# Two graph layers on one core: divisors of two relations in one reciprocal, asked for and applied at other places

## The chip, the cores and the metric

The kernel runs on one NeuronCore of a Trainium2 chip. The metric is the device time of one execution in microseconds. PE is the matrix engine, DVE the vector engine, ACT the scalar engine, POOL the GpSimd engine, and SP the engine whose queue issues most of the loads. Matmuls write into eight PSUM banks; what they leave there is read by ACT or DVE.

## The reference, cut to what matters

Node features of 384 nodes go through a graph attention layer, and then, after a layer norm and a rectification, through a relational network with two convolutions, 768 features, six relations and four bases per convolution. Only the convolution matters here.

```python
W = jnp.einsum('rb,bio->rio', comp, basis)
h_all = jnp.einsum('ni,rio->rno', x, W)
counts = jnp.zeros((R, n), x.dtype).at[edge_type, dst].add(1.0)
norm = 1.0 / counts[edge_type, dst]
msg = h_all[edge_type, src] * norm[:, None]
agg = jax.ops.segment_sum(msg, dst, num_segments=n)
return agg + x @ root + bias
...
x = jax.nn.relu(x)
x = x + h_in
x = _batchnorm(x, bn_gamma[l], bn_beta[l])
```

Each relation's messages are divided by the number of edges of this relation that end in the target node.

## The kernel before

The work stands in one program whose order is written out by hand: PE, POOL, SP, DVE and, after the first projection, ACT take their instructions in the order in which the program names them.

**The adjacency.** The tile `A` holds for each of the six relations a matrix of edge counts, source nodes on the partitions (3 blocks of 128) and 384 target nodes along the row, so that `A[:, r]` has 128 x 1152 numbers. It comes from memory, written there by scatters, relation by relation. For each relation `add_up(r)` on POOL adds the three blocks of sources into `sums[r]`, a slot of `sum_room` (128 x 384). `share(r)` turns this into the divisors. A matmul with a matrix of ones (L411 and L412 in the profile's lines, named `ps_cnt`) adds over the partitions and leaves the count of each target in all 128 partitions. Two ACT instructions (L414, L415) make max(count - 1, 0) + 1 of it, DVE takes the reciprocal (L416) and multiplies `A[:, r]` by it (L417). The divisors alternate between slots 4 and 5 of `sum_room`; the sums use slots 0 to 3, so that `add_up(4)` and `add_up(5)` wait until slots 0 and 1 have been read.

**The mixtures.** `mix(l, r, At, bs)` adds relation r, times its coefficient, onto `At[:, b]` for each basis b. For relation 0 it writes, on ACT (L396); for the others it adds, on DVE (L398). All of it must be done before the aggregation multiplies `At` with the transformed features.

**The bases.** Features times basis b gives `H_[:, b]`. Bases 0 and 1 of layer 0 are multiplied by a scheme of 15 products. Bases 2 and 3 use one of fewer products on halves. For each of them PE first runs three parts c=0, 1, 2 of 12 matmul instructions each (L1245), which fill the banks pe, pf, pb and pa. Then come the products with S[0], S[1], S[3] and S[2], of 6 instructions each (L1239): the S[0] and S[3] products in bank pc, the S[1] and S[2] products added onto bank pa. Between them ACT and DVE read out what has come together so far: ACT copies pa to `hs[0][0]` (L1251) before the S[1] product may add onto it, and again after it (L1258); DVE adds pb (L1252) and later products (L1260, L1262). The last product, `rest`, adds onto pa in part c=0 of the next basis, and ACT reads it (L1266). The sums of weights for the next basis (L1034, L1036) are made on DVE right after L1262, the fourth sum of weights (L1042) after the `rest`. Then follow the root matmuls (L1282), sums of the mixed adjacency (L1142) and of the features (L1365), and the aggregation (L1348), whose results DVE adds onto the features (L1375).

**What is put between.** `go_between(l, b, c)` is called after each part c of basis b, and with c=4 after the basis's products and the next basis's weight sums. What is done there is listed in `between`: shares of relations 0, 1, 2 after the parts of basis 2, share 3 and the mixture of relation 0 at (0, 2, 4), shares 4 and 5 after the first two parts of basis 3, and all mixtures of relations 1 to 5 at (0, 3, 4), ahead of the root matmuls.

**Banks.** `next_bank` takes the bank that was taken longest ago of those allowed. A matmul into a bank waits until what the bank held has been read.

```python
ps = next_bank("ps_cnt", [i for i in range(8) if i not in taken])
...
pe, pf, pb, pc, pa = [next_bank("ps_g", [i for i in range(8) if i not in taken[-1:]])[:, :N]
                      for _ in range(5)]
taken[:] = ring[-5:]
```

For basis 2 these are, by following the ring through the program, banks 3, 4, 7, 5 and 6, so that its pa is bank 6.

**Loads.** The weights of a basis come in three parts of four loads each through five buffers (L135, on SP's queue); the root's three parts (L137) come behind basis 3's. A load waits in the queue until its buffer has been read for the last time.

Of the kernel before, what the change touches and what calls it, by code (L numbers as in the profile page):

```python
# [14 lines left out]
AF = mybir.ActivationFunctionType  # L15
ALU = mybir.AluOpType

P = 128
N = 384
NT = N // P  # L20
# [5 lines left out]
HD = D // H  # L26
# [5 lines left out]
R = 6  # L32
# [69 lines left out]
def gnn_kernel(ctx: ExitStack, tc: tile.TileContext, out, x, edges, chunks, cols, rows, small,  # L102
               wq, wk, wv, wiq, wik, wiv, wo, w_in, basis, thirds, root, root_thirds, w_out):
    nc = tc.nc
# [15 lines left out]
    def next_bank(name, among=range(8)):  # L120

        i = next(i for i in ring if i in among)
        ring.remove(i)
        ring.append(i)
        return bank(i, name)
# [57 lines left out]
    ones = const.tile([P, P], F32, name="ones")  # L183
    nc.gpsimd.memset(ones, 1.0)

    minus = const.tile([P, 1], F32, name="minus")
# [4 lines left out]
    ps = next_bank("ps_warm")  # L191
# [197 lines left out]
    A = None  # L389

    def mix(l, r, At, bs=range(B)):

        for b in bs:
            w = small_sb[:, 4 + (l * R + r) * B + b:][:, :1]
            if r == 0:
                nc.scalar.activation(At[:, b], A[:, r], AF.Identity, scale=w)  # L396
            else:
                nc.vector.scalar_tensor_tensor(At[:, b], A[:, r], w, At[:, b], ALU.mult, ALU.add)  # L398

    sums = {}  # L400
    taken = []

    def add_up(r):
        sums[r] = sum_room[:, r % 4]
        nc.gpsimd.tensor_tensor(sums[r], A[:, r, 0, :], A[:, r, 1, :], ALU.add)
        nc.gpsimd.tensor_tensor(sums[r], sums[r], A[:, r, 2, :], ALU.add)

    def share(r):

        ps = next_bank("ps_cnt", [i for i in range(8) if i not in taken])  # L410
        nc.tensor.matmul(ps[:, :N], ones, sums[r], start=True, stop=True)  # L411
        rn = sum_room[:, 4 + r % 2]  # L412

        nc.scalar.activation(rn, ps[:, :N], AF.Relu, bias=minus)  # L414
        nc.scalar.activation(rn, rn, AF.Identity, bias=ones[:, 0:1])  # L415
        nc.vector.reciprocal(rn, rn)  # L416
        nc.vector.tensor_tensor(A[:, r], A[:, r], rn[:, None, :].to_broadcast([P, NT, N]), ALU.mult)  # L417
        if r + 4 < R:
            add_up(r + 4)


    with ExitStack() as inner:
        ap = inner.enter_context(tc.tile_pool(name="attn", bufs=2))
# [67 lines left out]
        with tc.tile_pool(name="edge", bufs=1, side="right") as ep:  # L491
# [5 lines left out]
            with tc.manual_schedule(engines={mybir.EngineType.Activation}):  # L497
# [6 lines left out]
                half = lambda t: lambda j: x_sb[:, t, j * 512:(j + 1) * 512]  # L504
# [180 lines left out]
        At = late.tile([P, B, NT, N], F32, name="At")  # L685
        A = late.tile([P, R, NT, N], F32, tag="A", name="A")
        sum_room = late.tile([P, 6, N], F32, name="sum_room")
# [206 lines left out]
        for j in range(2):  # L894
            ps = next_bank("ps_y", range(1, 8))[:, :256]
            for k in range(KD):
                nc.tensor.matmul(ps, attT[:, k, 2 * P:], w_o[1][k // 4][:, k % 4, j * 256:(j + 1) * 256],
                                 start=(k == 0), stop=(k == KD - 1))
# [108 lines left out]
    with tc.tile_pool(name="conv", bufs=1) as cp:  # L1007
# [107 lines left out]
        def shares(*rs):  # L1115
            return lambda: [share(r) for r in rs]

        def mixes(l, r, *bs):
            return lambda: mix(l, r, At, bs)

        between = {(0, 2, 0): shares(0), (0, 2, 1): shares(1),
                   (0, 2, 2): shares(2), (0, 2, 4): lambda: [share(3), mix(0, 0, At)],
                   (0, 3, 0): shares(4), (0, 3, 1): shares(5),
                   (0, 3, 4): lambda: [mix(0, r, At) for r in range(1, R)],
                   (1, 0, 0): mixes(1, 0, 0, 1, 2, 3)}
        for i in range(10):
            between[1, (i + 1) // 3, (i + 1) % 3] = mixes(1, 1 + i // 2, *((0, 1), (2, 3))[i % 2])
# [93 lines left out]
        for l in range(L):  # L1221
# [7 lines left out]
            for b in range(0 if l else BY_15, B):  # L1229
# [12 lines left out]
                for c in range(3):  # L1242
                    for ps, n, i, o, first in ((pa, 0, 0, 0, True), (pe, 2, 0, 0, True), (pf, 2, 0, 1, True),
                                               (pb, 0, 1, 0, True), (pe, 2, 1, 0, False), (pf, 2, 1, 1, False)):
                        nc.tensor.matmul(ps, block(XT, n, i)[:, c], w[c][:, i, o * HC:(o + 1) * HC],  # L1245
                                         start=(first and c == 0), stop=(c == 2 and (i == 1 or ps is pa)))
# [33 lines left out]
            for k in () if l else range(KC):  # L1280
                for o in range(KC):
                    nc.tensor.matmul(pr[o], w[k // 2][:, k % 2, o * P:(o + 1) * P], XT[:, k, :], start=(k == 0),  # L1282
                                     stop=(k == KC - 1))
# [73 lines left out]
            def feature_sums(p):  # L1357

                s0, s1, s3 = spaces[p % 2 * 3:][:3]
                o0, o1 = 2 * p, 2 * p + 1  # L1360
                S.append((s0, s1, h(o1, 0), s3))
                for dst, x, y, op in ((s0, h(o1, 0), h(o1, 1), ALU.add), (s1, s0, h(o0, 0), ALU.subtract),
                                      (h(o1, 0), h(o0, 0), h(o1, 0), ALU.subtract),
                                      (s3, h(o0, 1), s1, ALU.subtract)):
                    nc.vector.tensor_tensor(dst, x, y, op)  # L1365
                    yield
# [33 lines left out]
            for p in range(pairs):  # L1400
                last = p == pairs - 1
                sums = iter(()) if last else feature_sums(p + 1)
# [94 lines left out]
        ps = [next_bank("ps_f") for _ in range(3)]  # L1497
# [107 lines left out]
```

## Time and profile before

| what | value |
|---|---|
| runs | 710.24, 716.94 and 717.36 us, median 716.94 us |
| profiled execution | 709.97 us, span 708.2 us, mean granted clock 0.996 |
| PE busy | 691.4 us, 98% of the span |
| DVE busy | 557.9 us, 79% |
| ACT busy | 162.9 us, 23% |
| POOL busy | 313.5 us, 44% |
| count matmuls L411 | 12 instructions, 486 ns median each |
| reciprocals L416 | 6 of 128 x 384, 2.55 us each, 415.7 to 446.2 us |
| shares L417 | 6 of 128 x 1152, 1.36 us each |
| mixtures L398, both layers | 40 of 128 x 1152, 1.41 us each |

The profile is one execution; its times are counted from the start of the span. The span is what lies between the first and the last instruction, and the execution's time is 1.8 us longer. An instruction's own duration can be longer than its share of the path, because successive instructions of an engine overlap a little. Basis 2 of layer 0 begins at 409 us, basis 3 at 431 us, the root at 454.7 us and the aggregation near 480 us.

### The profile page before, as it was taken

What the parts mean: (1) busy time and instruction counts of PE and PEld (TensorE: products, weight loads), DVE (VectorE), ACT (ScalarE), POOL (GpSimd) and SP (SyncE); (2) the same over time, 40 slices, a digit from 0 to 9 for tenths busy, and PEclk for the clock granted to TensorE, in tenths of its full rate; (3) what the DMA queues carried; (4) which work ended last, traced back from release to release, by engine and by line L of the source; (5) the groups of instructions that cost most, each with busy time, mean ns of one, the idle gap of its engine ahead of it and who ended that gap; (6) DMA issues with size and microseconds to landing.
All of it is one profiled execution on the core that took longest, in us unless ns stands there. A gap on an engine that the chain in (4) does not pass through costs nothing.

```text
span 708.2 us, 9470 instructions
## 1 busy us (share of the span) xinstructions
PE 691.4 (98%) x3324; PEld 541.1 (76%) x3324; DVE 557.9 (79%) x1381; ACT 162.9 (23%) x375; POOL 313.5 (44%) x242
## 2 busy tenths in 40 slices
PE   8999999999999999999999999999999999999995
PEld 7759999999997444478998855558975555899943
DVE  6887697968886799787667889798878679378866
ACT  3201111111111577510131124101131111110101
POOL 1366678778687787588786473000000000000004
PEclk9999999999999999999999999999999999999998
DMA  8887677372563622733524996321004223520002
GB/s 305 271 305 261 221 254 211 76 246 60 213 195 59 179 2 2 223 45 46 120 0 91 238 285 190 134 89 45 1 1 131 69 77 124 193 90 1 0 1 90
DMA packets 70478, 91.07 MB, mean 129 GB/s; under 512 B 23084, under 2 KB 52368, under 8 KB 70046
## 3 DMA queue, kind: packets, MB, share of 16 engines
q1 hardware_dynamic: 48414, 79.24, 33.0%
q0 software_dynamic: 21296, 9.60, 10.6%
q10 hardware_dynamic: 720, 1.62, 0.7%
q8 instruction: 26, 0.43, 0.2%
q14 instruction: 22, 0.18, 0.1%
HBM read 79.27 MB, written 11.16 MB: 128 GB/s over the span
## 4 chain that ended last, share of the span: by engine, by line
PE 81%; DVE 13%; ACT 2%; DMA 2%; issue 1%; SPq 0%; DVEq 0%; ACTq 0%
PE ps_k L452 10%; PE ps_g L1245 9%; PE ps_v L452 9%; PE ps_g L1239 8%; PE ps_c L1348 7%; PE ps_q L470 6%; PE ps_q L452 5%; PE ps_g L1095 4%; DVE At L398 4%; PE ps_y L452 3%; PE ps_x L452 3%; PE ps_c L1183 3%; PE ps_o L758 2%; PE ps_s L713 2%; PE ps_pT L747 2%; PE ps_v L636 2%
## 5 line engine op out<-in xcount | busy, mean ns | idle before, releaser
L333 POOL DMA_INDIRECT atab<-count,at x99 | 166.2, 1679 | 49.2 <-DMA atab<-count,at 23.2
L328 POOL DMA_INDIRECT mtab<-m_val,at x99 | 104.6, 1057 | 54.9 <-issue 24.1
L1478 POOL TENSOR_TENSOR hf<-hf,room 128x512 f32<-128x512 f32 x3 | 4.3, 1421 | 257.8 <-ACT hf L1476 257.8
L398 DVE SCALAR_TENSOR_TENSOR At<-A,small_sb,At 128x1152 f32<-128x1152 f32 x40 | 53.6, 1413 | 0.0
L1245 PE MATMUL ps_g<-w_c,XN 128*128 128x384 f32 x144 | 47.7, 487 | 1.1 <-DVE XN L1375 1.1
L470 PE MATMUL ps_q<-hT,w_q 128*128 128x384 f32 (+1 forms) x160 | 41.8, 422 | 1.4 <-ACT hT L151 1.4
L1245 PEld LDWEIGHTS ps_g<-w_c,XN 128*128 128x128 f32 x144 | 27.3, 190 | 20.2 <-DVE XN L1375 1.4
L470 PEld LDWEIGHTS ps_q<-hT,w_q 128*128 128x128 f32 x160 | 28.5, 190 | 14.1 <-ACT hT L151 1.7
L1348 PE MATMUL ps_c<-At,H 128*128 128x192 f32 x216 | 36.7, 326 | 0.0
L1348 PEld LDWEIGHTS ps_c<-At,H 128*128 128x128 f32 x216 | 35.3, 190 | 0.5 <-DVE XN L1375 0.2
L452 PE MATMUL ps_k<-T,S 128*128 128x192 f32 x192 | 35.1, 326 | 0.0
L452 PEld LDWEIGHTS ps_k<-T,S 128*128 128x128 f32 x192 | 31.8, 190 | 0.0
L726 DVE CUSTOM_DVE_ANT_0 s<-ps_s,mask 128x384 f32<-128x384 f32 x48 | 24.5, 549 | 5.1 <-PE ps_s L713 5.1
L317 DVE SCALAR_TENSOR_TENSOR same<-cells,own,later 128x128 f32<-128x128 int32 x99 | 27.9, 348 | 0.4
L317 DVE SCALAR_TENSOR_TENSOR same<-keys,key,weigh 128x128 f32<-128x128 int32 x99 | 27.9, 349 | 0.0
L1239 PE MATMUL ps_g<-room,x_all 128*128 128x384 f32 x72 | 25.2, 486 | 0.0
L1245 PE MATMUL ps_g<-w_c,XT 128*128 128x384 f32 x72 | 24.3, 487 | 0.6 <-DVE H L1101 0.6
L1282 PE MATMUL ps_c<-XT,w_c 128*128 128x384 f32 x72 | 23.5, 486 | 0.0
L758 PE MATMUL ps_o<-At,v 128*64 128x384 f32 x96 | 20.8, 512 | 1.3 <-ACT attT L761 1.3
L713 PE MATMUL ps_s<-k,q 64*128 64x384 f32 x96 | 21.5, 528 | 0.0
L1245 PEld LDWEIGHTS ps_g<-w_c,XT 128*128 128x128 f32 x72 | 13.6, 190 | 10.3 <-DVE H L1101 1.0
L1239 PEld LDWEIGHTS ps_g<-room,x_all 128*128 128x128 f32 x72 | 13.7, 190 | 9.5
(386 smaller groups left out, 1556.7 us busy)
## 6 DMA issues: line engine op xcount, KB each, us to landing
w_c<-in_basis SPq DMA_DIRECT2D x72, 192.0 KB, 4.5
atab<-zero SPq DMA_DIRECT2D x36, 192.0 KB, 4.9
A<-atab POOLq DMA_DIRECT2D x12, 576.0 KB
keys<-keys_d SPq DMA_DIRECT2D x25, 192.0 KB, 5.0
w_c<-in_thirds SPq DMA_DIRECT2D x24, 192.0 KB, 3.6
w_q<-in_wiq SPq DMA_DIRECT2D x16, 256.0 KB, 5.8
w_k<-in_wk SPq DMA_DIRECT2D x16, 256.0 KB, 4.5
w_k<-in_wik SPq DMA_DIRECT2D x16, 256.0 KB, 4.2
```

Of the source, the lines that this page charges most:

```text
L317: nc.vector.scalar_tensor_tensor(same, row[:, n, :], mine[:, c:c + 1], times, ALU.is_equal, ALU.mult, accum_out=count[:, i, c:c + 1])
L328: nc.gpsimd.indirect_dma_start(mtab[c // PER][:, :], bass.IndirectOffsetOnAxis(at[:, 0, c:c + 1], 0), m_val[:, c:c + 1], None)
L333: nc.gpsimd.indirect_dma_start(atab[0 if i < 11 else i % 2][:, :], bass.IndirectOffsetOnAxis(at[:, 1, c:c + 1], 0), count[:, 1, c:c + 1], ...
L398: nc.vector.scalar_tensor_tensor(At[:, b], A[:, r], w, At[:, b], ALU.mult, ALU.add)
L452: nc.tensor.matmul(ps, a[:, k, :], b[:, k, :], start=start and k == 0, stop=(k == 3), skip_group_check=not start)
L470: nc.tensor.matmul(ps[o][:, c], wt_[:, k, o * P:(o + 1) * P], src[:, k, c], start=(k == 0 and c.start == 0), stop=(k == KD - 1 and c.stop ...
L713: nc.tensor.matmul(score[g][j][:, :N], q2[ho, hc, t * P:(t + 1) * P], k2[ho, hc, :], start=True, stop=True)
L758: nc.tensor.matmul(pso[p][j * HD:(j + 1) * HD, :N], v2[:, m, h * HD:(h + 1) * HD], turned(g)[:, j, :], start=(m == 0), stop=(m == NT - 1))
L1095: nc.tensor.matmul(ps, x[:, j], w[:, j], start=start and j == 0, stop=(j == 2), skip_group_check=not start)
L1239: nc.tensor.matmul(ps, x[:, c], y(c), start=start and c == 0, stop=(c == 2), skip_group_check=not start)
L1245: nc.tensor.matmul(ps, block(XT, n, i)[:, c], w[c][:, i, o * HC:(o + 1) * HC], start=(first and c == 0), stop=(c == 2 and (i == 1 or ps is ...
L1348: nc.tensor.matmul(ps, x[:, c], y[:, c], start=start and c == 0, stop=stop and c == 5, skip_group_check=True)
```

## The change

The six calls of `share` become three calls of `count_shares`, each for two relations, and six calls of a `share` that only multiplies. `count_shares(r)` adds the counts of relation r into partitions 0 to 63 of one bank and those of relation r + 1 into partitions 64 to 127, by two matmuls with 64 columns of ones. The two ACT instructions and the reciprocal then run once over both. Three ACT copies of 64 partitions spread each half over all 128 partitions, the second relation into slot 5 and the first into slot 4 of `sum_room`. The places change, too: the first count is at (0, 2, 2), its shares at (0, 2, 4), and so on. Of the mixtures of relation 1, two are at (0, 3, 0) and two at (0, 3, 1); those of relations 2 to 5 stay at (0, 3, 4).

```diff
+    def count_shares(r):
+
+        ps = next_bank("ps_cnt", [i for i in range(8) if i not in taken])
+        for j in range(2):
+            nc.tensor.matmul(ps[j * HD:(j + 1) * HD, :N], ones[:, :HD], sums[r + j], start=True, stop=True)
+        both = sum_room[:, 4]
+        nc.scalar.activation(both, ps[:, :N], AF.Relu, bias=minus)
+        nc.scalar.activation(both, both, AF.Identity, bias=ones[:, 0:1])
+        nc.vector.reciprocal(both, both)
+        for half in range(2):
+            nc.scalar.copy(sum_room[half * HD:(half + 1) * HD, 5], both[HD:, :])
+        nc.scalar.copy(both[HD:, :], both[:HD, :])
+        for j in range(2):
+            shared[r + j] = sum_room[:, 4 + j]
+            if r + j + 4 < R:
+                add_up(r + j + 4)
+
     def share(r):
-
-        ps = next_bank("ps_cnt", [i for i in range(8) if i not in taken])
-        nc.tensor.matmul(ps[:, :N], ones, sums[r], start=True, stop=True)
-        rn = sum_room[:, 4 + r % 2]
-
-        nc.scalar.activation(rn, ps[:, :N], AF.Relu, bias=minus)
-        nc.scalar.activation(rn, rn, AF.Identity, bias=ones[:, 0:1])
-        nc.vector.reciprocal(rn, rn)
-        nc.vector.tensor_tensor(A[:, r], A[:, r], rn[:, None, :].to_broadcast([P, NT, N]), ALU.mult)
-        if r + 4 < R:
-            add_up(r + 4)
-
+        nc.vector.tensor_tensor(A[:, r], A[:, r], shared.pop(r)[:, None, :].to_broadcast([P, NT, N]), ALU.mult)
...
-        between = {(0, 2, 0): shares(0), (0, 2, 1): shares(1),
-                   (0, 2, 2): shares(2), (0, 2, 4): lambda: [share(3), mix(0, 0, At)],
-                   (0, 3, 0): shares(4), (0, 3, 1): shares(5),
-                   (0, 3, 4): lambda: [mix(0, r, At) for r in range(1, R)],
+        between = {(0, 2, 2): lambda: count_shares(0),
+                   (0, 2, 4): lambda: [share(0), share(1), count_shares(2), mix(0, 0, At)],
+                   (0, 3, 0): lambda: [mix(0, 1, At, (0, 1)), share(2), share(3)],
+                   (0, 3, 1): lambda: [count_shares(4), mix(0, 1, At, (2, 3))],
+                   (0, 3, 2): shares(4, 5),
+                   (0, 3, 4): lambda: [mix(0, r, At) for r in range(2, R)],
```

More of the change, by code (lines that the diff above doesn't have):

```diff
@@ L406, in add_up @@
         nc.gpsimd.tensor_tensor(sums[r], sums[r], A[:, r, 2, :], ALU.add)
-    def share(r):
-        ps = next_bank("ps_cnt", [i for i in range(8) if i not in taken])
-        nc.tensor.matmul(ps[:, :N], ones, sums[r], start=True, stop=True)
-        rn = sum_room[:, 4 + r % 2]
-        nc.scalar.activation(rn, ps[:, :N], AF.Relu, bias=minus)
-        nc.scalar.activation(rn, rn, AF.Identity, bias=ones[:, 0:1])
-        nc.vector.reciprocal(rn, rn)
-        nc.vector.tensor_tensor(A[:, r], A[:, r], rn[:, None, :].to_broadcast([P, NT, N]), ALU.mult)
-        if r + 4 < R:
-            add_up(r + 4)
+    shared = {}
+    def count_shares(r):
[13 more added lines that the diff above has]
+                add_up(r + j + 4)
+    def share(r):
+        nc.vector.tensor_tensor(A[:, r], A[:, r], shared.pop(r)[:, None, :].to_broadcast([P, NT, N]), ALU.mult)
     with ExitStack() as inner:
```

## The prediction

> **What bounds the kernel now.** I read the page first: which engine is busy, and which one the chain that ended last runs through.
>
> ```profile
> PE 691.4 (98%) x3324; PEld 541.1 (76%) x3324; DVE 557.9 (79%) x1381; ACT 162.9 (23%) x375; POOL 313.5 (44%) x242
> PE 81%; DVE 13%; ACT 2%; DMA 2%; issue 1%; SPq 0%; DVEq 0%; ACTq 0%
> ```
>
> PE sets the time nearly everywhere; ACT is idle three quarters of it. So what an edit takes from DVE or adds to ACT matters only where PE waits for it. The change lies between 409 us (basis 2 of layer 0 begins) and 491 us. Next, the chain in order of time there:
>
> ```profile
> 430.61 0.66 PE ps_cnt L411 x2
> 431.29 0.59 ACT sum_room L414
> 431.90 0.62 ACT sum_room L415
> 432.52 4.58 ACT At L396 x4
> 437.11 0.48 ACT H L1266
> 437.72 0.88 PE ps_cnt L411 x2
> ...
> 454.76 0.55 DVE H L1262
> 455.32 15.95 DVE At L398 x12
> ```
>
> The chain leaves PE twice: for ACT at 431 us, where the mixture of relation 0 stands in the queue before the copy L1266, and for DVE after 454.76 us, through the mixtures. Then the timelines of ACT and PE, with what ended a wait in brackets:
>
> ```profile
> 422.89 0.58 ACT L414 ACTIVATE sum_room<-ps_cnt,minus 128x384 f32<-128x384 f32 x1 [3.29 <-PE ps_cnt L411]
> 423.50 0.62 ACT L415 ACTIVATE sum_room<-sum_room,ones 128x384 f32<-128x384 f32 x1
> 424.03 0.46 ACT L1251 COPY H<-ps_g 128x384 f32<-128x384 f32 x1
> ...
> 437.72 0.88 PE L411 MATMUL ps_cnt<-sum_room,ones 128*128 128x384 f32 x2 [0.66 <-ACT H L1266]
> ```
>
> L1251 reads pa, whose last matmul is among the first of part c=2, which began at 418.17. The copy could have run at about 419; it ran at 424.03, right behind L415. So ACT takes its instructions in the order of the program, and a copy behind a waiting one waits too. The PE line shows a count matmul held 0.66 us for a PSUM bank that L1266 had not yet read. Last, the DVE and PE lines where the mixtures are due:
>
> ```profile
> 424.15 2.55 DVE L416 RECIPROCAL sum_room<-sum_room 128x384 f32<-128x384 f32 x1 [0.51 <-ACT sum_room L415]
> 455.24 26.67 DVE L398 SCALAR_TENSOR_TENSOR At<-A,small_sb,At 128x1152 f32<-128x1152 f32 x20
> 491.02 2.22 PE L1348 MATMUL ps_c<-room,x_all 128*128 128x192 f32 x12 [0.78 <-DVE XN L1375]
> ```
>
> **The change, part by part.** I work it out as times of the profiled execution (span 708.2, whole 709.97 us), with its rows: 12 matmuls of 384 columns 3.87 us, 6 of them 1.94, two count matmuls 0.65, reciprocal 2.55, share 1.36, one mixture on DVE 26.58/20 = 1.33, one on ACT 4.58/4 = 1.15 to 1.24.
>
> *Count matmuls.* Before, the six pairs took 4.14 us (0.65, 0.65, 0.64 of path, then 0.66, 0.88, 0.65), and one waited 0.64 by the chain. After, three groups of four instructions on 64 columns of ones. The same shape is L758, 128*64 on 128x384, four of which take 0.80 us: 3 x 0.80 = 2.40. If the halves didn't run side by side, four would cost 1.30, 3.9 in all. I take 0.80, from the same shape.
>
> *First new wait.* count_shares(0) stands at (0,2,2), just ahead of L1251 in the program. PE: c=0 from 409.04 to 413.18, c=1 and c=2 to 420.92, counts to 421.72, S[0] product to 423.66. ACT: Relu and Identity from 421.75 to 422.98. DVE, free since 415.73: reciprocal to 425.56. Then ACT has three copies of 64x384, a form that the trace lacks. The bounds are 0.37 us (step between successive PSUM copies, L1254 to L1255) and 0.62 (L415, SBUF to SBUF); I take 0.53, nearer to the SBUF row, so 1.6 together, to 427.2. Only now comes L1251, to 427.56. Behind it on PE waits the S[1] product, which adds onto the bank that L1251 reads: 427.6 instead of 423.66, a stall of 3.9 us (3.4 to 4.2).
>
> *Second new wait.* PE: S[1], S[3], S[2] end at 433.42, counts of relations 2 and 3 at 434.22. DVE: L1262 to 434.0, six weight sums at 1.47 a pair (the last pair before, 435.53 to 437.00) to 438.4. Here SP's queue enters: the third part of basis 3 is loaded once PE's S[3] product has freed a buffer. That issue was at 427.41 and its data were used at 435.53 without a wait; it now comes some 3 us later, and landing takes 4.8 us in the median, 8.2 at most. Bounds 0 and 4 us, taken 0.3, so 438.7. The two root loads behind it keep their distance to PE. Then share(0) to 440.05 and share(1) to 441.4. Relu of the new count writes the row of divisors that share(0) reads, so it starts at 440.1; Identity ends at 441.3, reciprocal at 444.0, three copies at 445.6, the four ACT mixtures at about 450.2, L1266 at 450.7. PE meanwhile: c=0 and the rest of basis 2 to 440.03, c=1 to 443.9, then the count matmuls of relations 4 and 5. Their bank follows from the ring of banks. At the first count it reads, oldest first, 0, 1, 2, 3, 4, 7, 5, 6, and the last is basis 2's pa. Taken in turn, the first count gets bank 0, the second bank 1, basis 3 takes 2, 3, 4, 7, 5, and the oldest bank that the counts may take is 6: that pa, which L1266 has to read first. It is the wait that now costs 0.66 us. It becomes 450.75 - 443.9 = 6.85 us (6 to 10).
>
> *Third.* The last reciprocal starts about 452.85, the copies end at 457.0, L1251 of basis 3 at 457.4; PE is ready at 457.36. Cost 0.1. DVE's mixtures of relation 1 wait for ACT's at 446.9 to 448; behind them are share(2), share(3), which Relu awaits, already counted.
>
> *Ahead of the root.* PE ends basis 3 at 463.27 instead of 454.74: 2.40 + 3.94 + 6.85 + 0.09 - 4.14 - 0.64 = +8.5 us.
>
> *Mixtures moved up.* Four of DVE's twenty are gone from the end. DVE: L1262 at 463.85, 16 x 1.33 to 485.1, four share sums 5.2, four feature sums 3.6, one take: 494.2. PE, without waits, reaches the product now at 491.02 after 34.9 us (25.16 root and rest, 7.8, 1.95): 498.2. It took 36.28 us; that is -1.4, and DVE is early by 4. This is all that the move can give, since PE is next.
>
> *At no cost.* Three reciprocals saved (7.65 us of DVE): DVE isn't the bound before 455. Pool's sums of relations 4 and 5 are asked for after the first counts (421.7), but waited for DMA until 427.67 and 431.87 and end at 434.2, ten us before use; without that cover a late sum would add its own delay.
>
> *The clock.* 8.5 - 1.4 = +7.1 at full clock. Two stalls of 3.9 and 6.85 us have no like in the trace's middle (longest PE wait 1.4 us), but the two ends show what idling does: first the granted clock, third from the right, after the last matmul had ended at 700.50; then the warm-up matmuls, whose count per us is in brackets.
>
> ```profile
> 702.50:703.00 0.50, 0.00 (x0) 0.00 (x0) 0.50 (x2) 0.00 (x0) 0.00 (x0) 0.99 0.00 0
> 703.00:703.50 0.50, 0.00 (x0) 0.00 (x0) 0.46 (x3) 0.00 (x0) 0.00 (x0) 0.50 0.00 0
> ...
> 5.20:6.20 1.00, 1.00 (x7) 1.00 1.01 414
> 7.20:8.20 1.00, 1.00 (x12) 1.00 1.05 346
> ```
>
> 2.5 us of idle PE halved the clock, and the first 5 us of matmuls ran 7 a us where 12 came later (the clock column says 1.00 there; the pace does not). A stall then costs 0 to 5 x 5/12 = 2.1 us more. I take 2.1 for the second, well past 2.5 us, and half for the first, which is close to it: 3.15. [...]
>
> **Sum.** +10.3 us: 720.3 for the profiled execution. That one lies 7.0 below the median of 716.94 us (runs of 710.24 to 717.36), so on the median 727.2. The forecast's own range is +6 (full clock, short copies, low counts) to +14 (late load, both cold starts).
>
> **Rivals.**
> 1. Only one stall. If the bank of the third count is another, the second falls away: 10.3 - 6.85 - 2.1 = +1.4, 718.3 on the median; if the first is lost instead, 10.3 - 3.9 - 1.05 = +5.3, 722.3. For it: the banks are in no view, I followed them through the ring. Against it: by the same ring the count at 437.72 gets bank 6, and the trace shows just that wait.
> 2. The other side: ACT's copies don't hold back L1251 and L1266, because the divisors come before PE needs those banks. Then only the gains are left: 2.40 - 4.14 - 0.64 - 1.4 = -3.8, 713.1. It decides if reciprocal and copies are done by 423.66, 1.9 us after the counts. For it: DVE is idle there and PE has a 1.94 us product for cover. Against it: 0.6 + 0.6 + 2.55 + 1.6 = 5.4 us.
> 3. Deeper: the third weight part lands 4 us late and shares and mixtures slip behind it, with both cold starts: +15, 732.
>
> **How the numbers follow.** Forecast 0.70, rival 1 0.15, rival 2 0.10, rival 3 0.05. A measurement tells about 1% (7.2 us). Of the forecast 0.58 lies above that and 0.12 within (full clock, 7.1, is on the line). Slower: 0.58 + 0.05 = 0.63. Within: 0.12 + 0.15 + 0.05 = 0.32. Faster: half of rival 2, 0.05, by the spread of runs. The range goes from 714 (rival 1, or the forecast's low end on an execution like the profiled one) to 732.
>
> **What would show it.** In the profile after: PE idle some 4 us before an L1239 product near 424, released by ACT's L1251, and 6 to 7 us before a count matmul near 444, released by L1266; granted clock under 1.00 behind them; L1348 without waits. If PE's idle time between 409 and 463 stays under 2 us, the forecast is wrong; if it waits as told but the time rises by less than 5 us, the tail gave more than 1.4.

## The result, and the profile after

The changed kernel took 723.38 us in the median of eight runs (721.86 to 727.06), the kernel before 715.44 us in eight runs made beside it (710.24 to 717.36). The ratio of their means is 1.013, with a 95% interval of 1.0093 to 1.0167: slower by a little over 1%, and clear of the noise. The profiled execution of the changed kernel took 721.97 us with a span of 720.2, so 12.0 us more than the profiled one of before.

The page after, its lines on the engines and on the chain:

```profile
PE 695.0 (97%) x3324; PEld 541.7 (75%) x3324; DVE 547.4 (76%) x1378; ACT 163.7 (23%) x378; POOL 311.1 (43%) x242
PE 84%; DVE 10%; ACT 3%; DMA 2%; issue 1%; SPq 0%; DVEq 0%; ACTq 0%
```

DVE lost 10.5 us of work and its part of the chain fell from 13% to 10%, yet the span grew. PE's busy time rose by 3.6 us, although its count matmuls became cheaper (0.79 us for two relations, 421.04 to 421.83, where one took 0.65 before); where that comes from, the clock shows further down. In the lines below, the code after the edit stands up to ten lines further down: L1249 is what was L1239, L1255 was L1245, L1261 was L1251, L1276 was L1266, and the counts are L414, the copies of the divisors L420 and L421. PE's waits, in the view of who waited for whom (us in total, times, longest):

```profile
PE ps_cnt L414 <- ACT H L1276: 6.3, 1, 6.3
PE ps_g L1249 <- ACT H L1261: 3.9, 1, 3.9
```

Where they lie, in PE's timeline (start, duration, and in brackets the idle time and what ended it):

```profile
421.83 2.20 PE L1249 MATMUL ps_g<-room,x_all 128*128 128x384 f32 x6
427.95 4.21 PE L1249 MATMUL ps_g<-mroom,x_all 128*128 128x384 f32 x6 [3.91 <-ACT H L1261]
...
443.55 4.03 PE L1255 MATMUL ps_g<-w_c,XT 128*128 128x384 f32 x12
453.92 1.55 PE L414 MATMUL ps_cnt<-sum_room,ones 128*64 128x384 f32 x4 [6.33 <-ACT H L1276]
455.39 5.27 PE L1255 MATMUL ps_g<-w_c,XT 128*128 128x384 f32 x12
460.50 2.10 PE L1249 MATMUL ps_g<-room,x_all 128*128 128x384 f32 x6
```

From 421.83 to the next product it took 6.12 us, where 2.04 are enough when nothing waits (e2_first below, 457.95 to 459.99), and from 443.55 to the third count 10.37 us, where 3.96 are enough (e3_second, 443.66 to 447.62): two gaps of 4.08 and 6.41 us. Behind each, PE is slow as well. The 18 instructions from 427.95 to the second count at 436.85 took 8.90 us, 5.90 in e2_first; the counts and part c=2, from 453.92 to 460.50, took 6.58 us, 4.77 in e3_second. ACT's timeline names the reason for the gaps:

```profile
425.82 1.03 ACT L420 COPY sum_room<-sum_room 64x384 f32<-64x384 f32 x2 [2.62 <-DVE sum_room L418]
426.88 0.51 ACT L421 COPY sum_room<-sum_room 64x384 f32<-64x384 f32 x1
427.41 0.48 ACT L1261 COPY H<-ps_g 128x384 f32<-128x384 f32 x1
...
443.28 0.58 ACT L416 ACTIVATE sum_room<-ps_cnt,minus 128x384 f32<-128x384 f32 x1 [10.61 <-DVE A L428]
...
448.72 4.69 ACT L396 ACTIVATE At<-A,small_sb 128x1152 f32<-128x1152 f32 x4
453.32 0.45 ACT L1276 COPY H<-ps_g 128x384 f32<-128x384 f32 x1
```

L1261 and L1276 are the copies that PE needs. The first starts the moment the last divisor copy is through, the second when the last mixture is. The Relu at 443.28 had waited for DVE's share. And the clock, third number from the right of each stretch, first around the first gap, then around the second:

```profile
426.00:427.00 1.00, 0.00 (x0) 0.00 (x0) 0.00 (x0) 0.96 (x3) 1.00 (x2) 1.00 1.18 207
427.00:428.00 1.00, 0.05 (x1) 0.06 (x1) 0.07 (x1) 0.98 (x3) 0.76 (x1) 0.50 0.73 124
...
433.00:434.00 1.00, 1.00 (x3) 0.48 (x2) 0.00 (x0) 0.00 (x0) 0.92 (x2) 0.59 0.00 0
```

```profile
450.00:451.00 1.00, 0.00 (x0) 0.00 (x0) 0.99 (x1) 1.00 (x1) 0.00 (x0) 0.94 0.00 0
...
457.00:458.00 1.00, 1.00 (x4) 0.57 (x3) 1.00 (x1) 0.00 (x0) 0.00 (x0) 0.64 0.00 0
```

The clock fell to half at 427.0, 3.0 us after PE's last matmul had ended (421.83 + 2.20), and, by the share of its slice (0.94), at 450.9, 3.3 us after the last one there (443.55 + 4.03). It came back at 433.8 and 457.7 (0.59 and 0.64 of their slices). Last, the end of the stretch, in the timelines of DVE and PE:

```profile
468.92 21.35 DVE L398 SCALAR_TENSOR_TENSOR At<-A,small_sb,At 128x1152 f32<-128x1152 f32 x16
503.42 0.35 DVE L1385 TENSOR_TENSOR XN<-XN,ps_c 128x192 f32<-128x192 f32 x1 [4.09 <-PE ps_c L1358]
```

```profile
503.15 2.11 PE L1358 MATMUL ps_c<-room,x_all 128*128 128x192 f32 x12
```

Sixteen mixtures instead of twenty, and PE's product at 503.15 no longer waits; now DVE waits 4.09 us for PE. The product at 503.15 is the aggregation's with T2, one of the sums of the mixed adjacency, which stood at 491.02 us before, with a wait of 0.78 us.

To compare executions I take one number from PE's timeline, called the stretch: from the first matmul of basis 2 to the product with T2. It is 491.02 - 409.04 = 81.98 us before and 503.15 - 409.23 = 93.92 us after, so +11.94; what follows it takes 217.2 us before and 217.1 after.

### The profile page after: what moved, and what is told of

It is laid out like the page before. It is cut to its first block, busy times and chain, and to the rows that moved or that the text cites. A ratio compares the mean times of both kernels' runs of the same rounds, so it can differ in the third digit from the quotient of the medians.

```text
span 720.2 us, 9472 instructions
## 1 busy us (share of the span) xinstructions
PE 695.0 (97%) x3324; PEld 541.7 (75%) x3324; DVE 547.4 (76%) x1378; ACT 163.7 (23%) x378; POOL 311.1 (43%) x242
## 3 DMA queue, kind: packets, MB, share of 16 engines
q0 software_dynamic: 21296, 9.60, 10.5%
## 4 chain that ended last, share of the span: by engine, by line
PE 84%; DVE 10%; ACT 3%; DMA 2%; issue 1%; SPq 0%; DVEq 0%; ACTq 0%
PE ps_k L460 10%; PE ps_g L1255 9%; PE ps_v L460 8%; PE ps_g L1249 8%; PE ps_c L1358 8%; PE ps_q L478 6%; PE ps_q L460 5%; PE ps_g L1103 4%; PE ps_y L460 3%; PE ps_c L1292 3%; PE ps_x L460 3%; PE ps_c L1193 3%; PE ps_o L766 2%; PE ps_s L721 2%; PE ps_pT L755 2%; PE ps_v L644 2%
## 5 line engine op out<-in xcount | busy, mean ns | idle before, releaser
L1255 PE MATMUL ps_g<-w_c,XN 128*128 128x384 f32 x144 | 47.7, 487 | 1.1 <-DVE XN L1385 1.1
L1255 PEld LDWEIGHTS ps_g<-w_c,XN 128*128 128x128 f32 x144 | 27.3, 190 | 20.2 <-DVE XN L1385 1.4
L1255 PE MATMUL ps_g<-w_c,XT 128*128 128x384 f32 x72 | 25.3, 508 | 0.6 <-DVE H L1109 0.6
L1249 PE MATMUL ps_g<-room,x_all 128*128 128x384 f32 x72 | 25.3, 487 | 0.0
L1255 PEld LDWEIGHTS ps_g<-w_c,XT 128*128 128x128 f32 x72 | 14.1, 199 | 12.0 <-issue 2.1
L1249 PEld LDWEIGHTS ps_g<-room,x_all 128*128 128x128 f32 x72 | 13.6, 190 | 9.9 <-issue 0.6
```

What stands on the lines that cost most here:

```text
L1249: nc.tensor.matmul(ps, x[:, c], y(c), start=start and c == 0, stop=(c == 2), skip_group_check=not start)
```

## The experiments

The theory is that of the prediction: PE waits for two ACT copies that stand behind the new divisors' chain in the program's order, and idling costs clock on top. Each experiment takes away one part. The lines shown are from PE's timeline unless said otherwise; line numbers shift with each edit, and the engine and tile in brackets tell which copy ended a wait. Around e1_bank, e2_first, e4_warm and e5_mix_back, and around e8_before and e9_move_again, all kernels lost time long ahead of the stretch: in these traces the attention scores begin at 249 to 265 us instead of 225, and the kernel before took 744 us in the median beside the first four and 750 us beside the other two. So for these only the stretch is compared, and the spans expected for them can't be judged.

**e1_bank: only the bank of the third count.**

```diff
-        ps = next_bank("ps_cnt", [i for i in range(8) if i not in taken])
+        ps = next_bank("ps_cnt", [i for i in range(8) if i not in taken and (r, i) != (4, 6)])
```

> The changed kernel, with the third count matmuls kept off bank 6, so that they don't wait for the copy of the rest product. Theory (ACT's order holds PE; the bank is only the place where it shows): the count is no longer late, but Relu of that count still stands behind share(2), which ends near 454.0, then Identity, reciprocal 2.55 and three copies 1.54, so the copy of pa for basis 3 ends near 459.9 instead of 461.5 and PE waits some 5.5 us for it, cold clock again. Span within 1.5 us of the changed kernel's 720.2. Rival (the bank is the cause): the 6.33 us and the 1.9 us of half clock behind them go, span about 712.

```profile
475.83 0.87 PE L414 MATMUL ps_cnt<-sum_room,ones 128*64 128x384 f32 x4
...
488.43 4.10 PE L1249 MATMUL ps_g<-mroom,x_all 128*128 128x384 f32 x6 [5.73 <-ACT H L1261]
```

The third count (475.83) doesn't wait any more, and 12.6 us later PE waits 5.73 us for the copy of pa instead. The stretch is 92.39 us, 1.53 less than 93.92, of which 1.20 us are a shorter cold clock behind the first gap (457.46 to 465.16, 7.70 instead of 8.90 us). So the wait moved on; the bank was the place of it, ACT's queue the cause: L1261 starts at 487.89 us, right behind the last divisor copy (487.36, 0.51 us).

**e2_first: the first pair's copies behind the copies that PE needs.** `spread` makes the three copies, which `count_shares(r, True)` leaves out. The diff shows the places alone.

```diff
-        between = {(0, 2, 2): lambda: count_shares(0),
-                   (0, 2, 4): lambda: [share(0), share(1), count_shares(2), mix(0, 0, At)],
+        between = {(0, 2, 2): lambda: count_shares(0, True),
+                   (0, 2, 4): lambda: [spread(0), share(0), share(1), count_shares(2), mix(0, 0, At)],
```

> The changed kernel, with the three copies of the first pair of divisors moved from (0, 2, 2) to (0, 2, 4), behind the copies that read out basis 2; nothing else moves. Theory: the first stall of 3.91 us goes, and with it the half clock behind it, which cost 18 matmul instructions 3.1 us (8.90 instead of 5.81); the second stall stays and is up to 1.5 us longer, since the weight sums then fall beside Pool's sums. Span 713 to 715. Rival (the half-width count matmuls or the three copies by themselves are what costs): the copies are still made, and the span stays within 1.5 us of 720.2.

```profile
459.99 2.10 PE L1255 MATMUL ps_g<-mroom,x_all 128*128 128x384 f32 x6
...
482.94 1.55 PE L414 MATMUL ps_cnt<-sum_room,ones 128*64 128x384 f32 x4 [6.31 <-ACT H L1282]
```

The first gap is gone, the second is still 6.31 us long. The stretch is 87.26 us, 6.66 less, though the same copies are made. The gap and the half clock behind it had come to 4.08 + 3.00 = 7.08; behind the second gap the counts and part c=2 took 7.02 us here instead of 6.58, 0.44 more.

**e3_second: the later pairs' copies and the mixture of relation 0 moved back.**

```diff
-                   (0, 2, 4): lambda: [share(0), share(1), count_shares(2), mix(0, 0, At)],
-                   (0, 3, 0): lambda: [mix(0, 1, At, (0, 1)), share(2), share(3)],
-                   (0, 3, 1): lambda: [count_shares(4), mix(0, 1, At, (2, 3))],
-                   (0, 3, 2): shares(4, 5),
-                   (0, 3, 4): lambda: [mix(0, r, At) for r in range(2, R)],
+                   (0, 2, 4): lambda: [share(0), share(1), count_shares(2, True)],
+                   (0, 3, 0): lambda: [mix(0, 0, At), spread(2), mix(0, 1, At, (0, 1)), share(2), share(3)],
+                   (0, 3, 1): lambda: [count_shares(4, True), mix(0, 1, At, (2, 3))],
+                   (0, 3, 4): lambda: [spread(4), share(4), share(5)] + [mix(0, r, At) for r in range(2, R)],
```

> The changed kernel, with the copies of the second and third pair and the mixture of relation 0 put behind the copies that PE waits for; the first pair stays as it was. Theory: the first stall of 3.9 us stays, with a cold start of 1.9 to 3.1 us behind it; the second of 6.3 us and its cold start of 1.9 go, and the third doesn't turn up: stretch from the first matmul of basis 2 to the product with T2 85.0 to 86.5 us (changed kernel 93.92). Rival (the wait moves on to basis 3, as it did when the bank alone was changed): 91 to 93 us.

```profile
429.36 3.79 PE L1254 MATMUL ps_g<-mroom,x_all 128*128 128x384 f32 x6 [3.92 <-ACT H L1266]
...
447.62 0.87 PE L414 MATMUL ps_cnt<-sum_room,ones 128*64 128x384 f32 x4
```

The first wait, of 3.92 us, is all that is left; the third count has none. The stretch is 495.16 - 410.64 = 84.52 us, 9.40 less and 0.5 under what was expected, since the cold start behind the first gap cost 7.59 - 5.90 = 1.69 us this time. The time was 714.48 us in the median, 1.0031 of before (1.0001 to 1.0061). Taken away one at a time, the two give 6.66 and 9.40 us, together more than the 11.94 lost: 1.31 of the 9.40 are the shorter cold start in front, and the rest over 11.94, 2.8 us, are the gains of the edit, which come out from under the gaps. The copies and the mixture were moved at once, so what each of them is worth in the second gap isn't told apart.

**e4_warm and e4b_warm: PE kept busy in the gaps** by matmuls without use: 6 in the first gap and 10 in the second in e4_warm, 4 and 6 in e4b_warm, whose edit this is.

```diff
+        for _ in range({0: 0, 2: 0, 4: 6}[r]):
+            nc.tensor.matmul(bank(0, "ps_fill")[:, :N], ident, XT[:, 0, :], start=True, stop=True)
         ps = next_bank("ps_cnt", [i for i in range(8) if i not in taken])
...
+        for _ in range({0: 4, 2: 0, 4: 0}[r]):
+            nc.tensor.matmul(bank(2, "ps_fill")[:, :N], ident, XT[:, 0, :], start=True, stop=True)
```

> The changed kernel, with 6 matmuls of 128x384 without use behind the first count and 10 ahead of the third, 0.65 us each, 3.9 and 6.5 us, so that PE is busy where it waited. They are work on top of the reference's. Theory (idling itself halves the clock): granted clock 1.00 throughout, the 18 instructions behind the first stall take 5.8 us instead of 8.9 and the count and part c=2 behind the second 4.7 instead of 6.6; span 5.0 us shorter, about 715, although PE does 10.4 us of work more. Rival (PE is slow there because ACT, DVE and the transfers contend with it, or only the waits count): span 720 or longer.

In e4_warm the pace behind the gaps was the expected one (5.90 and 4.78 us, as in e2_first and e3_second; the clock there is not shown), but a filler took 0.93 us (5.60 for the first six), not 0.65, and both groups ran past the gaps: 93.85 us, as long as without them. What a warm PE is worth could not be read from that, so fewer were tried.

> The changed kernel, with matmuls of 128x384 without use in the two gaps, as before but 4 and 6 of them, since one took 0.93 us there instead of 0.65 and the fillers overran the gaps. They are work on top of the reference's. Theory (idling itself halves the clock): granted clock 1.00, the 18 instructions behind the first gap in 5.8 us and count and part behind the second in 4.7 us, the gaps no longer than 4.2 and 6.5 us; stretch 89 us instead of 93.92, so 5 us less for 9.4 us of added matmuls. Rival (PE is slow behind the gaps for another reason): the pace stays at 7.7 to 8.9 us, stretch 93 us or more.

```profile
429.38 2.20 PE L1253 MATMUL ps_g<-mroom,x_all 128*128 128x384 f32 x6 [0.36 <-ACT H L1265]
...
435.38 0.87 PE L416 MATMUL ps_cnt<-sum_room,ones 128*64 128x384 f32 x4
...
454.58 0.87 PE L416 MATMUL ps_cnt<-sum_room,ones 128*64 128x384 f32 x4 [2.96 <-ACT H L1280]
```

```profile
428.00:434.00 6.00, 5.64 (x19) 3.04 (x18) 0.93 (x2) 2.90 (x7) 3.25 (x3) 1.00 1.01 223
456.00:464.00 8.00, 7.94 (x25) 4.41 (x24) 7.20 (x5) 4.14 (x10) 0.00 (x0) 1.00 0.00 0
```

The clock stays at 1.00. The 18 instructions behind the first gap take 6.00 us instead of 8.90 (429.38 to 435.38), count and part behind the second 4.77 instead of 6.58. That is the 4.7 us of the cold clock, got back by adding work. The stretch is 91.66 us, 2.26 less, but not 89: DVE's weight sums for basis 3, asked for 1.5 us sooner, took 6.51 us instead of 4.38 (435.96 to 442.47), so the second gap grew by 2.1 us. Of that, 0.36 us are a wait for the third weight part; the rest is that three of the six sums took 1.24 to 1.46 us instead of 0.56 and 0.95. In the kernel before such sums took 1.24 and 1.75 us at 432.11 and 433.27, while Pool was adding up (431.87 to 434.21); what Pool did at these times in e4b_warm and what the cause was are not shown. In the time of the whole kernel (720.84 us, 1.0125 of before, 1.0069 to 1.0181) the gain over the changed kernel's 1.013 doesn't show.

**e5_mix_back: the mixtures of relation 1 back at (0, 3, 4).** The calls of `mix(0, 1, ...)` leave the two earlier places and the range there starts at 1 again.

> The changed kernel, with the mixtures of relation 1 put back to (0, 3, 4): the new divisors without the move. Theory: the two stalls stay as they are (3.9 and 6.3 us), the twenty mixtures end late again, and the product that took 34.9 us from the root's start takes about 36.3: span 1.4 us longer, 721.6. Rival (the mixtures on DVE between the parts add to the second stall by delaying share(2) or Relu): the span gets shorter, by up to 2.7 us.

The waits are 3.91 and 6.33 us as before the experiment. From the root's first matmul to the product with T2 it takes 543.35 - 506.90 = 36.45 us, against 34.91 in the changed kernel and 36.46 before (454.56 to 491.02): the move is worth 1.5 us, and it adds nothing to the gaps. The stretch is only 0.30 us longer (94.22), because PE's slow pace behind the first gap cost 7.70 - 5.90 = 1.80 us (467.85 to 475.55) instead of 3.00 in this execution.

**e6_both: neither gap.** As e2_first and e3_second together, and the divisors of later pairs in the slots of the sums just counted.

```diff
-        both = sum_room[:, 4]
+        both = sum_room[:, {0: 4, 2: 2, 4: 0}[r]]
```

> The changed kernel, with the three copies of each pair of divisors made after the copies that read out the basis, the mixture of relation 0 moved behind the rest product of basis 2, and the divisors of the later pairs in the slots of the sums that have just been counted, so that no Relu waits for a share. Theory: neither stall is left, granted clock 1.00; the stretch from the first matmul of basis 2 to the aggregation product with T2 is 78.5 us (before 81.98, changed kernel 93.92), the gains alone; time some 3.4 us or 0.5% under the kernel before. Rival (the halved counts or the nine copies cost something of their own on the path): stretch 82 us or more, not faster than before.

The two waits of PE in the stretch, from the view of who waited for whom:

```profile
PE ps_g L1261 <- DVE H L1116: 0.6, 1, 0.6
PE ps_c L1364 <- DVE XN L1391: 0.2, 1, 0.2
```

These are the only waits of PE's matmuls that the view lists in the stretch, 0.6 and 0.2 us; the first stands at its start and in the kernel before, too. The clock is 1.00 from 409 to 456 us. The stretch is 490.03 - 410.77 = 79.26 us, 2.72 under before and 0.8 over the 78.5 expected, most of it at the third counts (1.42 us up to the next matmul, 0.79 at the others), ahead of which Pool began its last sum late here: its first addition started at 438.66 us, after 4.83 us of waiting for the transfer, and took 1.82 us, where in the changed kernel it stood at 432.54 and took 0.99. That the counts were held by this sum is an estimate from these times. The time was 711.1 us against 711.9, a ratio of 0.9983 (0.9950 to 1.0015): 2.72 us are 0.4% of the whole, and the times alone don't tell that from nothing.

**e7_move_only and e9_move_again: the kernel before with only the mixtures of relation 1 moved up.**

```diff
-                   (0, 3, 0): shares(4), (0, 3, 1): shares(5),
-                   (0, 3, 4): lambda: [mix(0, r, At) for r in range(1, R)],
+                   (0, 3, 0): lambda: [share(4), mix(0, 1, At, (0, 1))], (0, 3, 1): lambda: [share(5), mix(0, 1, At, (2, 3))],
+                   (0, 3, 4): lambda: [mix(0, r, At) for r in range(2, R)],
```

> The kernel before, with one edit: the mixtures of relation 1 moved up, two behind share(4) at (0, 3, 0), two behind share(5) at (0, 3, 1). Theory: DVE falls behind by up to 5.3 us inside basis 3 but catches up most of it while it would wait for PE, the mixtures end some 3.6 us sooner, and PE loses its waits of 1.4 us ahead of the aggregation, but may wait some 0.5 us for the bank that DVE reads late: stretch 81.0 us, time 0.1% under before, within what can be measured. Rival (the DVE work put between holds PE inside basis 3): stretch over 82.5 us.

```profile
421.31 1.65 PE L411 MATMUL ps_cnt<-sum_room,ones 128*128 128x384 f32 x2 [3.56 <-POOL sum_room L406]
```

The stretch was 86.88 us, against the theory, but by a wait ahead of the edit: the second count stood 3.56 us for Pool's sum of relation 1, whose data had come late (Pool began to add at 418.21 us, at 412.04 in the first profile of before), and count and part c=2 behind it took 7.23 us, 4.52 in e9_move_again, so 2.71 of cold clock (0.60 in the mean from 421 to 428 us). Was that the edit? The same kernel and the one before were run once more.

> The kernel before with the mixtures of relation 1 moved up, once more. Theory (the wait for Pool's sum comes and goes with the transfers): without that wait the stretch is 80.6 us, 86.88 less 3.56 of wait and 2.71 of cold clock behind it. Rival (the edit brings the wait): 86 to 87 us again.

> The kernel before, once more, for a second profile of it. If the 3.56 us that PE waited for Pool's sum of relation 1 in the run with the mixtures moved up comes from transfers of that execution, and not from the edit (the program is the same up to there), the kernel before has it too in some executions: then its stretch is 87 to 88 us instead of 81.98 and its time 715 to 717. If it belongs to the edit, the stretch is 82 again in an execution of any length.

e9_move_again has no such wait, and its stretch is 80.43 us; e8_before has 81.98 us, the same as the first profile to the last digit. The 81.98 us alone would also fit a wait that the edit brings; that the edited kernel ran without it, and that it lies ahead of the edit in the program, speak for a wait of one execution. The move alone gives 1.55 us, with a time ratio of 1.0004 (0.9969 to 1.0040) in e7_move_only. Whether the spread of the kernel before, 710 to 717 us, comes from this late sum stays open: no profile of it has the wait.

## Why the prediction was right

Forecast were two waits and a cold clock, +10.3 us, 720.3 on the profiled execution and 727.2 on the median. The profile gives +12.0, and 721.97; the median is 723.38. By steps, from PE's timeline:

| step | predicted us | measured us |
|---|---|---|
| counts and the old bank wait | 2.40 - 4.78 = -2.38 | -1.81 |
| first gap | +3.94 | +4.08 |
| second gap | +6.85 | +6.41 |
| third gap | +0.1 | none (PE was slowed by the clock until then) |
| end of the mixtures | -1.4 | 34.91 - 36.46 = -1.55 |
| cold clock, first gap | +1.05 | 8.90 - 5.90 = +3.00 |
| cold clock, second gap | +2.1 | 6.58 - 4.77 = +1.81 |

The -1.81 are from e6_both, which has neither gaps nor cold starts: -2.72 of stretch, less -1.54 at the end (455.11 to 490.03, 34.92 us, against 36.46), less 0.63 for its longer third count. With these the measured sum is -1.81 + 4.08 + 6.41 - 1.55 + 3.00 + 1.81 = 11.94, as the stretch has it. At the end of the mixtures the prediction took 36.28 us from 454.74 on beside 34.9 that count from the root's first matmul; from that matmul, at 454.56, it is 36.46. The forecast was right in its mechanism, two waits for the two copies it named and a slow PE behind each, not only in its number; that its sum is off by no more than 1.7 us owes something to misses that go both ways. The places were right too: L1251's copy was predicted to end at 427.56 and ended at 427.89, the later copy of `rest` at 450.7 and ended at 453.77, of which some 3 us came from the first cold start, which shifted all behind it. The half-width counts took 0.79 us each at full clock, as the row of equal shape had said (0.80), and some 0.1 us more ahead of and behind each (in e3_second the parts around the third count took 3.96 and 3.97 us, 3.87 before), 0.6 in all, which it had not. The ACT copies, a form the trace of before lacked, took 0.51 us (0.53 taken).

Rival 1, one stall only, is out by the waits view, which has both, and e1_bank shows that a different bank would not have spared PE. Rival 2 is what e6_both had to be built for. Rival 3 did not come about, but its late weight part showed in e4b_warm as a wait of DVE of 0.36 us, near the 0.3 taken.

What was mis-sized is the term of the clock at the first gap. The prediction halved it, because 3.9 us of idling was close to the 2.5 us of the trace's end. In after, e1_bank and e3_second the clock fell there, at a cost of 3.00, 1.80 and 1.69 us, and in e5_mix_back, whose clock is not shown, the pace cost 1.80; the full 2.1 would have been nearer. Why the same gap costs so differently shows in the clock, here in the rows of e1_bank and of e3_second behind it:

```profile
458.00:463.00 5.00, 5.00 (x12) 2.77 (x11) 0.00 (x0) 1.04 (x3) 0.80 (x1) 0.66 0.00 1
```

```profile
428.00:434.00 6.00, 4.64 (x10) 2.66 (x11) 0.56 (x1) 2.88 (x7) 3.21 (x4) 0.72 0.87 143
```

A mean of 0.66 over 5 us, or of 0.72 over 6, is 3.4 us at half clock, if it fell to 0.50 as in after; in after it was 6.8 us (427.0 to 433.8, and 450.9 to 457.7). What a stall cost in clock is in these, to 0.1 us, half of the half-clock time in which PE was at work again: (433.8 - 427.95)/2 = 2.9 behind the first gap (3.00 measured), (457.7 - 453.92)/2 = 1.9 behind the second (1.81), 3.4/2 = 1.7 in e1_bank (1.80). So in after the longer gap cost less: more of the slow time went by while PE waited anyway (3.0 us against 1.0). In e1_bank the clock was still 1.00 up to 458.00 us, 0.5 us after PE had gone on (457.46). What sets the times at which the clock falls and comes back is not shown: no run here shifts a stall on purpose.

The other miss is the base. On the median the rise is 7.9 us, not 10.3, and the eight runs of before have a median of 715.44 us, not the 716.94 of the first three, so 727.2 was 3.8 too high. The eight runs of before spread over 7 us, those of after over 5, and the low ends lie 11.6 apart, as the profiles do. A sum from one profile should have been set beside runs at the same end. Why the runs of before spread more isn't shown. A late sum as in e7_move_only costs that program 3.56 + 2.71 = 6.3 us; the changed kernel asks for its first count only at 421.04 us, when even that late sum was all but done (421.25).

## What to carry to other kernels

ACT took its instructions in the order of the program here, and one that waited for another engine held back what stood behind it: the divisor copies waited 2.62 us for DVE, ran from 425.82 to 427.39 us, and only then, at 427.41, L1261. A change that splits a chain over engines should put its later half behind the copies that free the matmul banks, whatever the engine's idle share. Before moving such a chain, work out from the profile when each bank's next matmul is due: here ACT was idle 77% of the time, and a chain whose nine copies take 0.5 us each cost 15.3 us of waits and slow clock by its places (11.9 net of the gains), and nothing that shows once these were right. A stall of PE has to be priced with the slow pace after it, too: in the stretch it cost 1.7 to 3.0 us behind each wait of 3.56 us and more, with a mean clock of 0.50 to 0.72 where it was read, and nothing behind one of 2.96 us (e4b_warm, clock 1.00), while at the end of the trace of before 2.5 us without a matmul were enough for a clock of 0.50.

## What was not expected of the hardware

PE's idle gap and the pace after it can be traded: in e4b_warm ten matmuls without use shortened the real ones behind them by 4.7 us, of which 2.26 us were left in the stretch. These matmuls, each into the bank of the one before, took 0.92 and 0.94 us (3.66 us for the first four, 5.66 for the six) and not the 0.65 of the counts of the same shape in the kernel before; why is open.
